# A four-layer graph network on one core: halves of sums added on VectorE, plain transposes, and layer 1 as one stream

## The chip, the cores and the metric

The kernel runs on one core of a Trainium2 chip. The metric is the device time of one execution in microseconds (us). Before the change it is 849.05 us, the median of 3 runs (848.39 to 849.23). The profiled execution took 848.55 us; its trace spans 846.8 us at a mean granted TensorE clock of 0.988.

## The reference

There are 4096 nodes with 64 features, a 4096 x 4096 adjacency matrix of zeros and ones, and four layers. Each takes the normalised, rectified features and adds something aggregated over the neighbours.

```python
# layer 0: the last 100 neighbours of a row, each weighted by a power of 0.5
support = h @ weight
rank = jnp.cumsum(mask, axis=1); deg = rank[:, -1:]
k = jnp.minimum(deg, 100.0); pos = rank - (deg - k)
x = x + (mask * jnp.where(pos > 0, 0.5 ** (k - pos), 0.0)) @ support + bias
# layer 1: attention over the neighbours
h = lorentz_linear(h, W, b, scale)          # time = sigmoid(h[:, :1])*exp(scale)+1.1, rest rescaled
q = lorentz_linear(h, Wq, bq, scale_q); k = lorentz_linear(h, Wk, bk, scale_k)
qm = jnp.concatenate([-q[:, :1], q[:, 1:]], axis=-1)
att = adj * jax.nn.sigmoid((2.0 + 2.0 * (qm @ k.T)) / att_scale + att_bias)
support = att @ h
x = x + support / jnp.sqrt(clip(abs(-inner(support)), 1e-8))
# layer 2: two gated steps, each with m = adj @ (x @ W), then r, z, n as in a GRU
# layer 3: A @ (gamma * X) and A @ (gamma - 1) with hyperbolic rescaling before and after
# every layer: h = jnp.maximum(_layernorm(x), 0.0), and x = x + layer(h, adj)
```

## The kernel before

The adjacency matrix is held on chip transposed, in one-byte floats (`A8`), which is exact for zeros and ones. The output nodes are treated in four quarters `q` of 1024 nodes, each in two chunks `c` of 512; the sum over the source nodes runs over 32 blocks `b` of 128. A value of the features is split into three bf16 parts. The first two lie side by side in `hm` (128 columns), the third in `lo` (64 columns). A product with `hm` uses the full array, one with `lo` half of it ("tiled"); so one bank of sums holds two halves of 64 rows that must still be added.

TensorE's order is laid down when the program is built. A helper (`weave`) keeps a clock for each engine, and puts pre- and post-processing of other quarters (generators that `yield` one instruction after the other) in between the large products. It also draws on a background list: `checks`, VectorE instructions that test every half tile (128 x 512) of the adjacency in 32-bit form for values other than 0 and 1, by a separate load.

```python
def evac(acc, bias=None):                       # both banks to the on-chip buffer
    a = [b2(f"agg{c}", (P, CW)) for c in (0, 1)]
    if bias is None:
        S_.activation(a[0], acc[0], AF.Copy)
        V.tensor_copy(a[1], acc[1])
    else:
        S_.activation(a[0], acc[0], AF.Identity, bias=bias)
        V.tensor_scalar(a[1], acc[1], bias, None, op0=ALU.add)
    ...
def to_nm(a, kind):                             # to rows of nodes; adds the halves
    def half(ps, c):
        ps = bank(kind, "ps_n") if ps is None else ps
        for j in range(CB):                     # both = two 64x64 identities, one on the other
            mm(ps[:, (c * CB + j) * D:(c * CB + j + 1) * D], a[c][:, j * P:(j + 1) * P], both)
        return ps
    ps = yield PE([a[0]], lambda: half(None, 0), 0.8, [kind])
    yield PE([a[1]], lambda: half(ps, 1), 0.8)

# pre1(q): the queries, each block twice, so that both halves of the array find them
ys = [b2("q", (P, CB, 2, D)) for _ in range(2)]
for c in range(2):
    yield from stretch(hq, tm[:, QB:], f[:, QB:], ys[c], slice(c * CB, (c + 1) * CB), -1.0)
kT[q] = b2(f"kT{q}", (P, CW))
yield from transpose4(y, 1, kT[q])
for c in range(2):
    qd = b2("qd", (P, CW))
    yield from transpose4(ys[c].rearrange("p b t d -> p (b t) d"), 1, qd)
    ...                                         # and to DRAM

def stream1(q):                                 # layer 1, one quarter
    acc = [one(f"acc{c}") for c in (0, 1)]
    ...  # weigh(i, c): 2 score products, sigmoid on ScalarE, times A8 on VectorE
    behind = None
    for i in range(NB // 2):
        gs = []
        for c in (0, 1):
            gs.append(weigh(i, c)); weave.draw(c == 1 or weave.quiet)
        for c in (0, 1):
            if behind: add(c, *behind)          # the sums of the step before
            weave.draw(weave.quiet)
        behind = (i, gs)
        if i == 8: load1(q + 1)                 # the queries of the next quarter
    weave.finish()
    for c in (0, 1): add(c, *behind)
    return acc

def sum2(acc, layer, q, bs):                    # layer 2, eight blocks
    for b in bs:
        for c in (0, 1): add_hm(acc, layer, b, c, a8(q, b)(c), b == 0)     # full width
        weave.draw()
    for b in bs:
        for c in (0, 1): add_lo(acc, layer, b, c, a8(q, b)(c), b == NB - 1)  # half width
        weave.draw(False)
```

Layer 2 already takes the even blocks of nodes as one chunk and the odd ones as the other (`a8`), and adds the halves by `take2`: a copy of one half by ScalarE (`mt`), an addition by VectorE (`mx`). Layers 0 and 1 take the first and the last 512 nodes as chunks.

Of the kernel before, what the change touches and what calls it, by code (L numbers as in the profile page):

```python
# [790 lines left out]
def fast_kernel(ctx: ExitStack, tc: tile.TileContext, t: dict, out: bass.AP, flag: bass.AP):  # L791
# [76 lines left out]

    both = const.tile([P, D], F32, name="both")
    V.tensor_tensor(both, ident[:, :D], ident[:, D:], ALU.add)  # L870
# [66 lines left out]
    def book_pe(o, lhsT, rhs, passes):  # L937
        k, m, n = lhsT.shape[0], math.prod(lhsT.shape[1:]), math.prod(rhs.shape[1:])
        tiled = k < P or m < P
        dur = max(0.42e-3 * n * passes * (0.5 if tiled else 1.0), 0.09 * (2.0 if passes == 4 else 1.0))  # L940
        weave.book("P", dur + (0.115 if tiled != weave.tiled else 0.0), names(lhsT, rhs), names(o))
        weave.tiled = tiled
# [60 lines left out]
    def add_hm(acc, layer, b, c, rhs, first):  # L1003
        o = like(acc[c], rhs)
        mm(o, HM[layer, b // QB][:, b % QB, :], rhs, start=first, stop=False)
# [5 lines left out]
    def evac(acc, bias=None):  # L1011

        a = [b2(f"agg{c}", (P, CW)) for c in (0, 1)]
        if bias is None:
            S_.activation(a[0], acc[0], AF.Copy)
            V.tensor_copy(a[1], acc[1])
        else:
            S_.activation(a[0], acc[0], AF.Identity, bias=bias)
            V.tensor_scalar(a[1], acc[1], bias, None, op0=ALU.add)
        for ps in acc:  # L1020
            free(ps)
        return a

    def to_nm(a, kind):

        def half(ps, c):
            ps = bank(kind, "ps_n") if ps is None else ps
            for j in range(CB):
                mm(ps[:, (c * CB + j) * D:(c * CB + j + 1) * D], a[c][:, j * P:(j + 1) * P], both)
            return ps  # L1030
        ps = yield PE([a[0]], lambda: half(None, 0), 0.8, [kind])
        yield PE([a[1]], lambda: half(ps, 1), 0.8)
        return blocks(ps)

# [71 lines left out]
    def stream0(q):  # L1106
# [5 lines left out]
        def turn(b):  # L1112

            n = q * NB + NB - 1 - b
            a = A8[q][b // 2][:, b % 2, :]
            wt = b2("w", (P, 2 * CW), I16)
            for c in (0, 1):
                if b < NB - 1:
                    before = A8[q][(b + 1) // 2][:, (b + 1) % 2, :]
                    mm(cnt[c], upd, before[:, cols[c]], start=False, stop=False)  # L1120
                mm(cnt[c], tri, a[:, cols[c]], start=b == NB - 1, stop=b == 0)
# [35 lines left out]
        for b in range(1, NB, 2)[::-1]:  # L1157
# [18 lines left out]
            if b == NB // 2 + 1:  # L1176
                xq[q] = b2(f"x{q}")
                Y_.dma_start(xq[q], x_nm[:, q * QB:(q + 1) * QB, :])
        for x in cnt:
            free(x)  # L1180
        while waiting:
            for _ in sums():
                weave.draw()
# [38 lines left out]
    def stretch(h, tm, f, o, s, sign):  # L1222

        n, k = o.shape[1], o.shape[2]
        yield root[0].tensor_scalar(o[:, :, :, 0], tm[:, s, None].to_broadcast([P, n, k]), sign, None, op0=ALU.mult)
        yield DV.tensor_tensor(o[:, :, :, 1:], h[:, s, None, 1:].to_broadcast([P, n, k, D - 1]),
                               f[:, s, None, None].to_broadcast([P, n, k, D - 1]), ALU.mult)

    def pre1(q, X):
# [10 lines left out]
        every = slice(0, QB)  # L1240
        S1[q] = b2(f"S1_{q}")
        tm, f = yield from lorentz([hs], [es[:, 0:1]])
        yield from stretch(hs, tm, f, S1[q][:, :, None, :], every, 1.0)
# [17 lines left out]
        yield from stretch(hk, tm[:, :QB], f[:, :QB], y[:, :, None, :], every, 1.0)  # L1261
        ys = [b2("q", (P, CB, 2, D)) for _ in range(2)]
        for c in range(2):
            yield from stretch(hq, tm[:, QB:], f[:, QB:], ys[c], slice(c * CB, (c + 1) * CB), -1.0)
# [3 lines left out]
        for c in range(2):  # L1268
            qd = b2("qd", (P, CW))
            yield from transpose4(ys[c].rearrange("p b t d -> p (b t) d"), 1, qd)  # L1270
            q_spill[q, c] = dram.tile([P, CW], F32, name=f"qs{q}_{c}")
            yield AC.dma_start(q_spill[q, c], qd)
# [3 lines left out]
    def load1(q):  # L1276
        if q < NQ:
            qd[q] = [b2("qd", (P, CW)) for _ in range(2)]
            for c in range(2):
                Y_.dma_start(qd[q][c], q_spill[q, c])  # L1280

    def stream1(q):

        acc = [one(f"acc{c}") for c in (0, 1)]

        def weigh(i, c):
            kb = kT[i // 4][:, (i % 4) * P:(i % 4 + 1) * P]
            ps = two("score").rearrange("p (j n) -> p j n", j=2)
            for j in range(2):
                half = slice(j * D, (j + 1) * D)  # L1290
                mm(ps[:, j, :], kb[half, :], qd[q][c][half, :])
            g = b4p.tile([P, 2, CW], F32, tag="b4", name="sig")
            S_.activation(g, ps, AF.Sigmoid, bias=att_add, scale=att_mul)
            free(ps)
            V.tensor_tensor(g, g, A8[q][i][:, :, c * CW:(c + 1) * CW], ALU.mult)
            return g

        def add(c, i, gs):
# [5 lines left out]
        behind = None  # L1304
        for i in range(NB // 2):
            if q == 0 and i % (QB // 2) == 0:
                weave.until((1, i // (QB // 2)), DONE)
            weave.quiet = (1, NQ - 1) not in DONE
            weave.late = 2.0 if weave.quiet else 1.0
            gs = []  # L1310
            for c in (0, 1):
                gs.append(weigh(i, c))
# [495 lines left out]
```

## Time and profile before

| what | before |
|---|---|
| time, median of 3 | 849.05 us |
| layer 0 | from the start to 249.6 us |
| layer 1, four quarters | 252.3 to 517 us |
| layer 2, two steps | 518 to 727 us |
| layer 3 products | 727 to 821.8 us |
| rest after the last product of layer 3 | 25.0 us |
| VectorE busy in layer 1, one inner quarter | 54.4 of 64.4 us |

A line of the profile that tells of a group has the line of the program (here mostly a helper's), the engine, the operation, output and inputs by name, then shapes, and a count after "x". After the bar stand busy time in us and mean ns of one, then idle time of the engine before such instructions and who ended it. PE is TensorE, DVE VectorE, ACT ScalarE; PEld is the load of weights, which overlaps products. For TensorE the product's own duration is longer than the time until the next can start; what it costs in a row is seen from start to start. A 32-bit product makes two records, a transpose one.

### The profile page before, as it was taken

To read this page: it belongs to the slowest core of one execution; us is meant where nothing else is said; L and a number is where in the kernel's file an instruction comes from. 1 tells how busy PE (TensorE), PEld (TensorE's weight loads), DVE (VectorE), ACT (ScalarE), POOL (GpSimd) and SP (SyncE) were. 2 spreads that over 40 slices of the span, in tenths; PEclk is the share of its full clock that TensorE was granted. 3 is DMA by queue.
4 is the path that set the end of the run, shared out by engine and by line. 5 is a ranking of instruction groups with operands and counts; after the bars stand their busy time and mean duration, and the time that the engine had idled before them with its cause. 6 is when DMAs were issued, how large, how long until landed. Compare 5 with 4: busy or idle time off the path is not lost.

```text
span 846.8 us, 12798 instructions
## 1 busy us (share of the span) xinstructions
PE 803.9 (95%) x4682; PEld 378.5 (45%) x4682; DVE 644.0 (76%) x1670; ACT 397.8 (47%) x609; POOL 69.5 (8%) x143
## 2 busy tenths in 40 slices
PE   5999999999998999999999999999999999999980
PEld 2434434444442333333333334444444444699980
DVE  6725766667667888888888888977678788885996
ACT  5654555555546666666666663022210234452342
POOL 4333322322000000000000000000000000000000
PEclk9999999999999999999999999999999999999995
DMA  9999999999641041032022133796778920000010
GB/s 133 114 141 161 161 198 205 149 176 204 131 138 36 14 148 51 13 101 63 12 88 63 37 112 137 260 308 194 257 251 299 313 58 13 1 2 2 14 26 17
DMA packets 67752, 101.63 MB, mean 120 GB/s; under 512 B 18785, under 2 KB 35169, under 8 KB 67681
## 3 DMA queue, kind: packets, MB, share of 16 engines
q1 hardware_dynamic: 46800, 79.18, 29.9%
q0 software_dynamic: 18432, 16.79, 21.0%
q10 hardware_dynamic: 2448, 4.76, 1.6%
q8 instruction: 39, 0.64, 0.3%
q14 instruction: 33, 0.26, 0.1%
HBM read 144.75 MB, written 6.29 MB: 178 GB/s over the span
## 4 chain that ended last, share of the span: by engine, by line
PE 86%; DVE 7%; DMA 2%; ACT 2%; issue 1%; POOL 0%; POOLq 0%; ACTq 0%; DVEq 0%
PE acc L947 50%; PE score L947 14%; PE cnt L947 13%; PE ps_l L947 2%; PE ps_t L951 2%; PE rz L947 2%; DMA half<-in_adjT 2%; PE ps_n L947 2%; PE ih L947 1%; DVE sig L780 1%; DVE n L780 1%; DVE nt L780 1%; DMA A<-in_adjT 1%; PE ps_kq L947 1%; DVE rc L780 1%
## 5 line engine op out<-in xcount | busy, mean ns | idle before, releaser
L780 ACT ACTIVATE sig<-score,fatt_add,fatt_mul 128x1024 f32<-128x1024 f32 x128 | 147.6, 1199 | 86.3 <-PE score L947 85.6
L780 DVE TENSOR_TENSOR sig<-sig,A 128x1024 f32<-128x1024 f32 x128 | 151.3, 1221 | 37.1 <-ACT sig L780 36.6
L780 ACT ACTIVATE w<-cnt 128x512 int16<-128x512 f32 x192 | 108.1, 595 | 95.9 <-PE cnt L947 93.8
L947 PE MATMUL score<-qd,kT 64*128 64x512 f32 x512 | 128.0, 616 | 2.1 <-ACT sig L780 2.1
L947 PE MATMUL acc<-sig,S 128*64 128x512 f32 x512 | 125.1, 606 | 1.1 <-DVE sig L780 0.8
L947 PE MATMUL acc<-A,hm 128*128 128x512 fp8e4 x512 | 117.5, 380 | 0.9 <-DVE X L780 0.9
L947 PEld LDWEIGHTS <-hm 128*128 128x128 bf16 x768 | 72.4, 98 | 94.1 <-issue 18.4
L947 PE MATMUL cnt<-A,ftri 128*128 128x512 fp8e4 x256 | 98.1, 386 | 7.9 <-DMA A<-in_adjT 7.9
L780 DVE SCALAR_TENSOR_TENSOR half<-half 128x512 f32<-128x512 f32 x150 | 98.3, 683 | 2.6 <-DMA half<-in_adjT 2.6
L947 PE MATMUL cnt<-A,fupd 128*128 128x512 fp8e4 x248 | 95.6, 385 | 4.3 <-ACT w L780 2.1
L947 PE MATMUL acc<-S,A 128*128 128x196 bf16 x1024 | 88.5, 247 | 0.0
L947 PEld LDWEIGHTS <-A 128*128 128x128 fp8e4 x1024 | 87.2, 97 | 1.5 <-issue 1.0
L780 DVE TENSOR_SCALAR w<-cnt 128x512 int16<-128x512 f32 x64 | 44.2, 690 | 50.9 <-PE cnt L947 49.8
L947 PEld LDWEIGHTS score<-qd,kT 64*128 64x128 f32 x512 | 43.8, 186 | 79.5 <-ACT sig L780 36.9
L1104 POOL DMA_DIRECT2D A<-in_adjT x128 | 67.7, 531 | 138.5 <-DMA A<-in_adjT 135.1
L947 PE MATMUL acc<-w,hm 128*128 128x512 bf16 x256 | 75.1, 379 | 0.0
L947 PEld LDWEIGHTS acc<-sig,S 128*64 128x64 f32 x512 | 30.3, 136 | 83.2 <-issue 30.4
L780 DVE SCALAR_TENSOR_TENSOR whole<-whole 128x1024 f32<-128x1024 f32 x53 | 63.5, 1219 | 4.9 <-DMA whole<-in_adjT 4.3
L947 PEld LDWEIGHTS <-lo 128*64 128x64 bf16 x768 | 35.4, 109 | 59.8 <-issue 40.1
L947 PE MATMUL acc<-A,lo 128*64 128x512 fp8e4 x512 | 61.3, 382 | 0.0
L1561 POOL MEMSET S<- 128x4 bf16 x8 | 0.9, 119 | 545.5 <-DVE xT L780 481.0
L947 PEld LDWEIGHTS <-fupd 128*128 128x128 bf16 x248 | 24.6, 99 | 43.7 <-issue 21.7
(180 smaller groups left out, 724.2 us busy)
## 6 DMA issues: line engine op xcount, KB each, us to landing
half<-in_adjT SPq DMA_DIRECT2D x150, 256.0 KB, 6.6
whole<-in_adjT SPq DMA_DIRECT2D x53, 512.0 KB, 6.4
A<-in_adjT POOLq DMA_DIRECT2D x128, 128.0 KB, 12.7
x<-in_x SPq DMA_DIRECT2D x8, 256.0 KB, 16.1
qs<-qd ACTq DMA_DIRECT2D x8, 256.0 KB, 5.7
qd<-qs SPq DMA_DIRECT2D x8, 256.0 KB, 2.7
mx<-gs SPq DMA_DIRECT2D x16, 128.0 KB, 7.3
xT<-gs SPq DMA_DIRECT2D x8, 256.0 KB, 7.1
```

What stands on the lines that cost most here:

```text
L780: return fn(*args, **kw)
L947: nc.tensor.matmul(o, lhsT, rhs, start=start, stop=stop, skip_group_check=True)
L951: nc.tensor.transpose(o, src, ident)
L1104: nc.gpsimd.dma_start(A8[q][b // 2][:, b % 2, :], adjT[b * P:(b + 1) * P, q * 2 * CW:(q + 1) * 2 * CW])
L1561: nc.gpsimd.memset(S3[q, c][:, :, 3 * e:], 1.0)
```

## The change

Six things are changed, mostly to take work and waits from TensorE.

1. The halves of the sums of layers 0 and 1 are added as in layer 2: ScalarE copies the other half of each bank, VectorE adds. One tile holds both chunks, one in the upper and one in the lower 64 partitions, so four plain 128 x 128 transposes bring it to rows of nodes.
2. For that, layers 0 and 1 take even and odd blocks as chunks too.
3. The queries are turned once, not twice; the load from DRAM puts them on both halves of the partitions.
4. In layer 2 a piece of eight blocks starts with the half-width products if the array is in that tiling, to change it less often.
5. Layer 1 is one stream over its four quarters: the first scores of a quarter are issued before the last sums of the one before, and those of the first quarter before the last sums of layer 0.
6. The helper's own clock gets other figures for transposes, 32-bit products and changes of tiling.

```diff
     def evac(acc, bias=None):
-        a = [b2(f"agg{c}", (P, CW)) for c in (0, 1)]
-        if bias is None:
-            S_.activation(a[0], acc[0], AF.Copy)
-            V.tensor_copy(a[1], acc[1])
-        else:
-            S_.activation(a[0], acc[0], AF.Identity, bias=bias)
-            V.tensor_scalar(a[1], acc[1], bias, None, op0=ALU.add)
-        for ps in acc:
+        lo, hi = slice(0, D), slice(D, P)
+        a, mt = b2("agg", (P, CW)), b2("mt", (P, CW))
+        sides = ((lo, hi), (hi, lo))
+        for ps, (own, other) in zip(acc, sides):
+            S_.activation(mt[own, :], ps[other, :], AF.Copy)
+        for ps, (own, other) in zip(acc, sides):
+            if bias is None:
+                V.tensor_tensor(a[own, :], ps[own, :], mt[own, :], ALU.add)
+            else:
+                V.scalar_tensor_tensor(a[own, :], ps[own, :], bias[own, :], mt[own, :], op0=ALU.add, op1=ALU.add)
             free(ps)
     def to_nm(a, kind):
+        def run():
+            ps = bank(kind, "ps_n")
+            for j in range(4):
+                turn4(ps[:, j * P:(j + 1) * P], a[:, j * P:(j + 1) * P])
             return ps
+        ps = yield PE([a], run, 0.7, [kind])
 ... # stream0: a8(q, b) in place of columns c * 512 ...; before its last sums, in the last quarter:
+        if q == NQ - 1:
+            begin1()                    # weigh(0, 0, c) for both c, kept in `ahead`
 ... # pre1
-        ys = [b2("q", (P, CB, 2, D)) for _ in range(2)]
-        for c in range(2):
-            yield from stretch(hq, tm[:, QB:], f[:, QB:], ys[c], slice(c * CB, (c + 1) * CB), -1.0)
+        yq = b2("q")
+        yield from stretch(hq, tm[:, QB:], f[:, QB:], yq, -1.0)
 ...
+        qT = b2("qT", (P, CW))
+        yield from transpose4(yq, 1, qT)
 ... # load1
-                Y_.dma_start(qd[q][c], q_spill[q, c])
+                for half in (slice(0, D), slice(D, P)):
+                    Y_.dma_start(qd[q][c][half, :], q_spill[q][c * D:(c + 1) * D, :])
 ... # stream1
+        for q in range(NQ):
+            for i in range(NB // 2):
+                ...
+                gs = ahead[:] if (q, i) == (0, 0) else []
+                for c in range(len(gs), 2):
+                    gs.append(weigh(q, i, c))
+                    weave.draw(c == 1 or weave.quiet)
+                if behind:
+                    add_behind()        # after step 15: weave.finish(), evac, post1 of that quarter
+                behind.append((q, i, gs))
+        add_behind()
 ... # sum2: wide(stop) and narrow(stop) are the two loops of before
+        if weave.tiled and bs[0]:
+            narrow(False)
+            wide(True)
+        else:
+            wide(False)
+            narrow(True)
 ... # the helper's clock
-        dur = max(0.42e-3 * n * passes * (0.5 if tiled else 1.0), 0.09 * (2.0 if passes == 4 else 1.0))
-        weave.book("P", dur + (0.115 if tiled != weave.tiled else 0.0), names(lhsT, rhs), names(o))
+        dur = max(0.42e-3 * n * passes * (0.5 if tiled else 1.0), 0.09)
+        if passes > 1 and not tiled:
+            dur += 0.05 if passes == 2 else 0.075
+        weave.book("P", dur + ((0.18 if passes == 4 else 0.115) if tiled != weave.tiled else 0.0), ...)
```

## The prediction

> **What bounds the kernel now.** I read the page's busy times and its chain first, then the waits of TensorE, then the groups by shape, and last the timeline around every place that the change touches.
>
> ```profile
> PE 803.9 (95%) x4682; PEld 378.5 (45%) x4682; DVE 644.0 (76%) x1670; ACT 397.8 (47%) x609; POOL 69.5 (8%) x143
> PE 86%; DVE 7%; DMA 2%; ACT 2%; issue 1%; POOL 0%; POOLq 0%; ACTq 0%; DVEq 0%
> ```
>
> ```profile
> PE flag_ps L947 <- DVE odds L780: 18.5, 1, 18.5
> PE cnt L947 <- DMA A<-in_adjT: 7.9, 1, 7.9
> PE cnt L947 <- ACT w L780: 2.1, 7, 0.6
> ```
>
> TensorE is busy for 803.9 of 846.8 us. Its one long wait is at the end: its last sum of layer 3 ends at 821.8 us, and then 25 us of VectorE work (two last post-processings) remain. Before that it idles for 18 us in all, 7.9 of them at the start for the first adjacency block. So before 821.8 us a microsecond of TensorE work removed is a microsecond gained, if no wait takes its place, and the last 25 us stay. Here is what the pieces cost (mean ns after the busy time):
>
> ```profile
> L947 PE MATMUL ps_n<-both,agg 128*128 128x64 f32 x128 | 16.0, 277 | 1.5 <-ACT agg L780 1.5
> L951 PE MATMUL ps_t<-fident,q 128*128 128x128 f32 x32 | 4.9, 274 | 0.0
> L780 ACT ACTIVATE agg<-acc,W 128x512 f32<-128x512 f32 x4 | 2.7, 687 | 8.1 <-PE acc L947 8.1
> L780 DVE TENSOR_TENSOR mx<-acc,mt 64x512 f32<-64x512 f32 x16 | 11.0, 689 | 3.0 <-ACT mt L780 2.6
> L780 ACT ACTIVATE mt<-acc 64x512 f32<-64x512 f32 x16 | 9.5, 591 | 64.0 <-PE acc L947 63.6
> L780 DVE TENSOR_TENSOR q<-hq,f 128x504 f32<-128x504 f32 x8 | 5.4, 676 | 0.0
> ```
>
> Now a border between two quarters of layer 1 (start, length):
>
> ```profile
> 319.57 3.99 PE L947 MATMUL acc<-sig,S 128*64 128x512 f32 x16
> 323.49 1.99 PE L947 MATMUL score<-qd,kT 64*128 64x512 f32 x8
> 325.41 2.00 PE L947 MATMUL ps_n<-both,agg 128*128 128x64 f32 x16
> 327.33 1.99 PE L947 MATMUL score<-qd,kT 64*128 64x512 f32 x8
> ```
>
> A normal pair of steps is 1.92 us of scores and 1.87 of sums. The two groups of sums at the seam take 323.49 - 319.57 = 3.92 instead of 3.74: the seam costs 0.18 us, not a round trip through ScalarE and VectorE, because the sums of step 14 cover it. What is dear there is the 1.92 us of ps_n. The border between layers 0 and 1 is different:
>
> ```profile
> 249.00 0.62 PE L947 MATMUL acc<-w,lo 128*64 128x512 bf16 x4
> 250.40 2.00 PE L947 MATMUL ps_n<-both,agg 128*128 128x64 f32 x16 [0.77 <-ACT agg L780]
> 254.60 0.63 ACT L780 ACTIVATE sq<-xc 128x512 f32<-128x512 f32 x1 [4.26 <-DVE xc L780]
> 255.14 4.72 ACT L780 ACTIVATE sig<-score,fatt_add,fatt_mul 128x1024 f32<-128x1024 f32 x4
> 256.38 2.22 PE L947 MATMUL score<-qd,kT 64*128 64x512 f32 x8 [2.06 <-ACT sig L780]
> 259.39 2.21 PE L947 MATMUL acc<-sig,S 128*64 128x512 f32 x8 [0.79 <-DVE sig L780]
> ```
>
> TensorE has nothing to overlap with here: 0.77 + 2.06 + 0.79 = 3.62 us of it stand idle. Last, what a tiling change costs, in layer 0:
>
> ```profile
> 125.72 0.38 PE L947 MATMUL acc<-w,hm 128*128 128x512 bf16 x1
> 126.03 0.62 PE L947 MATMUL acc<-w,lo 128*64 128x512 bf16 x4
> 126.59 0.39 PE L947 MATMUL cnt<-A,fupd 128*128 128x512 fp8e4 x1
> ```
>
> A full-width product is followed by the next after 0.216 us; by a half-width one after 0.31. The way back costs as much: two pairs of half-width products would be 0.43 to 0.47 us and take 0.56. I take 0.1 us per change.
>
> **What the Trainium skill says.** "TensorEngine Tiling (Array Packing)", section "Tiling Modes", says that changing the tiling mode drains TensorE; the 0.31 against 0.216 above agrees. "TensorE: Matmul & The Clock Gate", section "Part 4: PE-mode transpose", gives about 275 ns for a 128x128 transpose inside a kernel; the records here say 274. But four in a row start 0.109 us apart, so the four hold TensorE for 0.44 us, and it is this that I count. "PSUM — Partial Sum Buffer", section "Specifications (TRN2)", says that a VectorE instruction may take at most one tensor input from PSUM: this is why adding two halves of a bank takes a copy by ScalarE first. No run here tests it; the trace shows layer 2 doing it in that way (mt, then mx). "DMA: Bandwidth & Descriptors", section "Rules for kernel authors", advises against splitting a transfer into two partition halves, because they serialize. The queries are now loaded so. The two loads of before land after 2.7 us and are asked for 8 steps (30 us) ahead, so I give this no cost.
>
> **The change part by part.**
>
> *Halves added on VectorE, plain transposes.* Per aggregate 16 ps_n records go. They hold TensorE for 1.84 us next to full-width work and for 1.92 us between half-width work. Four transposes come, 0.44 us, or about 0.52 with the change of tiling. This is 1.4 us for each of eight aggregates. The evacuation grows: instead of 0.69 on ScalarE beside 0.75 on VectorE, two copies of 0.59 on ScalarE and two adds of 0.69 on VectorE, the first add behind the first copy. From the end of the sum to the finished tile it is 0.6 + 0.7 + 0.7 = 2.0 us instead of 0.75. In layers 1 and 2 other products fill this: 4 x 1.4 = 5.6. At the end of layer 0 scores fill it: 1.4. At the three inner seams of layer 0 I expect most to be lost. There the next quarter starts with one block in flight, and its counts need the same two engines to empty the banks. At the seam at 190 us the first w leaves ScalarE at 191.7 and would now leave at 192.3; that of VectorE leaves at 192.0 and would leave at 193.1. Count products that started at 193.13 would start at 192.4 and 193.2, and the third block, which began at 194.41, at about 193.7, then stall once and take in the 0.44 of transposes. I count 0.35 x 3 = 1.0. Sum: 8.0 us.
>
> *Queries turned once.* Per quarter one set of four transposes less, three times 0.44 in layer 0 and once 0.52 in layer 1: 1.85 us. VectorE loses 4 x (0.68 + 0.17) and ScalarE 4 x 0.60; they are not the bound.
>
> *Start of layer 1.* The scores of the first step (8 records, 1.9 us) are issued before the last sums of layer 0, so their sigmoid and multiplication run under 1.5 us of sums and the next scores. Of 3.62 us idle I expect 3.0 back. Part may return: ScalarE's sq waited 4.26 us for VectorE ahead of the sigmoids, and this normalisation still has to be fitted in.
>
> *Seams inside layer 1.* 3 x 0.18 = 0.5 us. The fourth seam, after the last quarter, stays.
>
> *Fewer tiling changes in layer 2.* There are 2 steps x 4 quarters x 4 pieces = 32 pieces, each now wide-narrow, so nearly 2 changes a piece. Alternating, one stays inside each piece and most of the 31 between pieces go; eight pieces with block 0 must start wide, and gates and transposes in between force some. I take 20 changes x 0.1 = 2.0 us.
>
> *Even and odd blocks as chunks.* Layer 2 already streams this strided view at 0.216 us a product, so TensorE pays nothing. VectorE's multiplication reads A in runs of 128 instead of 512; I take it as unchanged at 1.22 us.
>
> Sum: 8.0 + 1.85 + 3.0 + 0.5 + 2.0 = 15.35 us, so 849.05 - 15.35 = 833.7 us.
>
> **Rivals.** (1) *The checks spill into the tail.* VectorE also tests all 256 half tiles of the adjacency for values other than 0 and 1, in gaps, at 0.61 us each. Layer 1 gets shorter and VectorE's own work grows by about 2 us (adds +5.3, queries -3.4), so some 10 checks move later. What is left at the end lies in the last 25 us: 10 left would cost 6 us, hence 840. Against it: before, checks are all but finished by 717 us, one 1.2 us and one 0.7 us piece remain, and the 200 us of layer 2 have VectorE 79% busy, so there is room. (2) *The seams of layer 0 get worse*: copies and adds ahead of the count evacuations on both in-order engines. If each seam loses 1 us instead of gaining 0.35, the time is 838. For it: the counts already wait 0.25 us there. Against: only the first two blocks are exposed. (3) *The start of layer 1 gains all and more*: with the two products ahead, the later single waits vanish too, and layer 0 loses its stray waits (1.78 us at 109 us). This makes 829 to 830. (4) *VectorE becomes the bound of layer 1*: 54.4 us of 64.4 in a quarter now, about 55 of 62.7 after; the checks give way first, so I think this unlikely; it would show as 835 to 838.
>
> **Range and chances.** 2% is 832.1 us, only 1.6 us below my number. The terms are each sure to about 1 us except the start of layer 1 and layer 0's seams (1.5 each), and program order moves everywhere, so stray waits of 1 to 2 us come and go. Range 828.5 to 839. Faster by over 2%: 0.32; within: 0.65; slower: 0.03.
>
> **What would show it.** ps_n as 32 transposes of 128x128 with some 4 us of TensorE in place of 16; records for q halved to 16; scores of layer 1 standing before the last lo products of layer 0; no gap of 2 us near 255; a full-width run of 32 hm products in layer 2; a quarter of layer 1 at about 62.7 us instead of 64.4; the last layer 3 product at about 806.5. I am wrong if checks stand in the last 25 us in number, if TensorE waits over 1 us at each layer 0 seam, or if multiplications of layer 1 take clearly more than 1.22 us.

## The result and the profile after

The changed kernel takes 839.36 us (median of 4 runs, 838.91 to 840.59), the kernel before beside it 849.14 us (848.39 to 850.65). The ratio is 0.9885, with a 95% interval of 0.9867 to 0.9902. The change saves 9.8 us; 15.35 were predicted, and 839.36 lies 0.4 us above the predicted range.

The page after, first the busy times, then the chain by engine:

```profile
PE 786.7 (94%) x4549; PEld 368.7 (44%) x4570; DVE 648.4 (77%) x1675; ACT 400.8 (48%) x613; POOL 69.5 (8%) x143
PE 82%; DVE 9%; DMA 5%; ACT 2%; issue 1%; SPq 0%; DVEq 0%
```

TensorE lost 17.2 us of busy time (803.9 before), more than was predicted (a few products are missing in this trace: 4549 against 4570 weight loads), but its share of the chain fell from 86 to 82% and that of DMA rose from 2 to 5%. So part of the removed work came back as waiting. The groups by shape show that the operations themselves changed as foreseen:

```profile
L780 DVE SCALAR_TENSOR_TENSOR agg<-acc,W,mt 64x512 f32<-64x512 f32 x8 | 6.0, 749 | 9.2 <-ACT mt L780 9.1
L950 PE MATMUL ps_n<-fident,agg 128*128 128x128 f32 x32 | 5.1, 281 | 0.0
L950 PE MATMUL ps_t<-fident,q 128*128 128x128 f32 x16 | 2.5, 276 | 0.0
```

ps_n is now 32 transposes, and the query transposes are halved to 16. The multiplication of layer 1 (`sig<-sig,A`), which now reads A in runs of 128, takes 1222 ns instead of 1221. To see where the gain is and where it isn't, I cut both traces at the same events: layer 0 ends with the start of its last count product, layer 1 with the first product of layer 2, layer 2 with the first of layer 3, layer 3 with the start of its last product; the tail is the rest.

| stage, us | before | after | difference | predicted |
|---|---|---|---|---|
| layer 0 | 247.0 | 252.2 | +5.2 | -2.3 |
| layer 1 | 269.6 | 262.6 | -7.0 | -9.6 |
| layer 2 | 210.9 | 204.6 | -6.3 | -3.4 |
| layer 3 | 94.1 | 93.9 | -0.2 | 0 |
| tail | 25.2 | 24.6 | -0.6 | 0 |

(The predicted column is the prediction's sum by place: in layer 0 the three seams, 1.0, and three query sets, 1.32; in layer 1 the 1.4 at its border, 3 of the 4 aggregates, 4.2, the start, 3.0, one query set, 0.5, and the seams, 0.5; in layer 2 the last aggregate, 1.4, and the tilings, 2.0.)

Layer 0 is where the largest surprise lies: it got longer. The waits of TensorE and of VectorE between 60 and 252 us, in the trace after (total, number, longest):

```profile
PE cnt L946 <- DVE w L780: 5.5, 2, 4.0
PE cnt L946 <- ACT w L780: 5.4, 7, 1.4
DVE half L780 <- DMA half<-in_adjT: 7.9, 3, 4.8
```

Before, the same three were 1.8, 1.4 and 2.6 us. The first and the third belong together, as the timeline after shows (start, length, in brackets the idle time before and who ended it):

```profile
112.24 0.69 DVE L780 SCALAR_TENSOR_TENSOR half<-half 128x512 f32<-128x512 f32 x1 [4.83 <-DMA half<-in_adjT]
...
112.86 0.69 DVE L780 TENSOR_SCALAR w<-cnt 128x512 int16<-128x512 f32 x1
```

```profile
113.60 0.59 PE L946 MATMUL cnt<-A,fupd 128*128 128x512 fp8e4 x1 [4.02 <-DVE w L780]
```

`half` is one of the background tests of the adjacency (`checks`, counted in half tiles below). VectorE kept to the order of the program here. It stood at a test whose load had not landed, and the evacuation `w` of a count bank stood behind it: TensorE's last product before had ended at 109.58 us, but `w` began at 112.86. TensorE waited 4.02 us for that bank. The granted clock went down with it; by the trace it was half from 112.15 to 118.97 us. Here are the window of 5 us with the stop in it and the next one (PEclk is the third number from the right, then DMA share and GB/s):

```profile
110.00:115.00 5.00, 1.04 (x4) 0.29 (x5) 2.13 (x6) 0.62 (x2) 1.05 (x2) 0.71 1.10 200
115.00:120.00 5.00, 5.00 (x16) 1.61 (x16) 3.16 (x15) 1.20 (x3) 1.58 (x3) 0.60 1.10 201
```

From 115 to 120 us TensorE never rests and finishes 16 products; before, at the same place, 29. The kernel before has the same stop in small (VectorE 2.59 us, TensorE 1.78 us at 109 us) and no drop of the clock after it. The DMA queues are full in both (share 1.10 in these windows). The two loads of tests on the chain after take 16.5 and 17.5 us, the one on the chain before 14.5 us.

The three inner seams of layer 0 show the second wait of the list:

```profile
70.07 1.21 ACT L780 ACTIVATE mt<-acc 64x512 f32<-64x512 f32 x2 [3.16 <-PE acc L946]
...
71.30 0.60 ACT L780 ACTIVATE w<-cnt 128x512 int16<-128x512 f32 x1
...
71.95 0.38 PE L946 MATMUL cnt<-A,fupd 128*128 128x512 fp8e4 x1 [1.37 <-ACT w L780]
```

The two copies of the evacuation occupy ScalarE ahead of the first `w`, and TensorE waits 1.37 us for it at each seam.

The start of layer 1:

```profile
253.32 1.99 PE L946 MATMUL score<-qd,kT 64*128 64x512 f32 x8
...
256.21 0.62 PE L946 MATMUL acc<-w,lo 128*64 128x512 bf16 x4
...
307.33 0.66 PE L950 MATMUL ps_t<-fident,k 128*128 128x128 f32 x4 [2.15 <-DVE k L780]
```

The scores stand before the last sums of layer 0, and the three waits of before (0.77, 2.06 and 0.79 us) are gone. But at step 12 of the first quarter, 50 us later, TensorE waits 2.15 us for `k`: the keys of the last quarter of nodes, which come out of the last sums of layer 0 by way of its post-processing and the normalisation of layer 1. In the trace before this wait does not exist.

Layer 2 after; each line is a run of full-width (hm) or half-width (lo) products:

```profile
582.51 3.64 PE L946 MATMUL acc<-A,lo 128*64 128x512 fp8e4 x32
586.09 7.08 PE L946 MATMUL acc<-A,hm 128*128 128x512 fp8e4 x32
```

Runs of 32 take the place of runs of 16: the trace has 42 changes of tiling in the whole of layer 2 instead of 70.

### The profile page after: what moved, and what is told of

It reads as the page before. It is cut to its first block, busy times and chain, and to the rows that moved or that the text cites. A ratio compares the mean times of both kernels' runs of the same rounds, so it can differ in the third digit from the quotient of the medians.

```text
span 837.9 us, 12661 instructions
## 1 busy us (share of the span) xinstructions
PE 786.7 (94%) x4549; PEld 368.7 (44%) x4570; DVE 648.4 (77%) x1675; ACT 400.8 (48%) x613; POOL 69.5 (8%) x143
## 4 chain that ended last, share of the span: by engine, by line
PE 82%; DVE 9%; DMA 5%; ACT 2%; issue 1%; SPq 0%; DVEq 0%
PE acc L946 50%; PE score L946 13%; PE cnt L946 11%; DMA half<-in_adjT 4%; PE ps_l L946 2%; DVE sig L780 2%; PE rz L946 2%; PE ih L946 2%; PE ps_t L950 1%; DVE nt L780 1%; DVE n L780 1%; DMA x<-in_x 1%; DVE ss L780 1%; ACT w L780 1%; ACT sig L780 1%
## 5 line engine op out<-in xcount | busy, mean ns | idle before, releaser
L780 DVE TENSOR_TENSOR sig<-sig,A 128x1024 f32<-128x1024 f32 x128 | 151.3, 1222 | 33.0 <-ACT sig L780 32.6
L946 PE MATMUL acc<-A,hm 128*128 128x512 fp8e4 x512 | 115.6, 379 | 0.0
L780 DVE SCALAR_TENSOR_TENSOR half<-half 128x512 f32<-128x512 f32 x156 | 101.5, 686 | 8.0 <-DMA half<-in_adjT 7.9
L946 PE MATMUL acc<-w,hm 128*128 128x512 bf16 x235 | 69.9, 382 | 0.7 <-issue 0.2
L946 PEld LDWEIGHTS <-lo 128*64 128x64 bf16 x768 | 36.9, 109 | 58.5 <-issue 36.7
L780 DVE SCALAR_TENSOR_TENSOR whole<-whole 128x1024 f32<-128x1024 f32 x50 | 59.8, 1219 | 3.0 <-DMA whole<-in_adjT 2.6
L946 PE MATMUL acc<-A,lo 128*64 128x512 fp8e4 x512 | 59.3, 380 | 0.0
L780 ACT ACTIVATE mt<-acc 64x512 f32<-64x512 f32 x32 | 18.9, 591 | 65.6 <-PE acc L946 65.2
L946 PEld LDWEIGHTS <-ftri 128*128 128x128 bf16 x256 | 25.0, 99 | 48.8 <-issue 26.9
```

The source lines that it names most:

```text
L780: return fn(*args, **kw)
L946: nc.tensor.matmul(o, lhsT, rhs, start=start, stop=stop, skip_group_check=True)
```

## The experiments

Three questions: do the tests take the gain back; what are the waits of layer 0 and of the start of layer 1 worth; and what do the single parts bring. The theory I began with was *room*: the 256 half tiles need a fixed amount of VectorE time, VectorE is busy for 225 of 262.6 us in layer 1 after (86%; before 224 of 269.6, 83%) and for 167 of 204.6 in layer 2 (82%), so time taken out of these layers takes room from the tests, and they are paid for in layer 0 or in the tail. The rival was that the change's own waits eat the gain, tests or no tests. The stages of the runs, with the tests that lie in each:

| run | time, us | layer 0 | layer 1 | layer 2 | tail | tests in layers 0, 1, 2, tail |
|---|---|---|---|---|---|---|
| before | 849.14 | 247.0 | 269.6 | 210.9 | 25.2 | 63, 42, 148, 3 |
| after | 839.36 | 252.2 | 262.6 | 204.6 | 24.6 | 74, 39, 143, 0 |
| b2_nochecks0 | 881.67 | 244.8 | 269.9 | 209.6 | 61.6 | 0, 44, 154, 58 |
| a2_nochecks0 | 885.75 | 244.9 | 263.8 | 205.7 | 75.6 | 0, 34, 144, 78 |
| b0_none | 841.85 | 244.8 | 268.5 | 208.2 | 24.4 | none |
| a0_none | 832.71 | 243.7 | 263.7 | 204.0 | 24.8 | none |
| a3_land | 861.32 | 245.8 | 263.8 | 205.8 | 50.4 | 40, 35, 140, 41 |
| a12_hl78 | 838.82 | 245.3 | 263.7 | 205.8 | 28.8 | 67, 37, 146, 6 |
| a10_late_hland | 841.51 | 243.0 | 263.2 | 205.7 | 33.9 | 63, 35, 144, 14 |
| a9_late_aland | 840.61 | 244.0 | 263.2 | 205.7 | 31.7 | 65, 35, 144, 12 |
| a6_late | 844.24 | 252.3 | 263.2 | 205.7 | 28.1 | 74, 34, 144, 4 |
| a1_oldclock | 842.76 | 247.2 | 264.8 | 206.5 | 29.1 | 69, 35, 147, 5 |
| a4_nobegin | 841.82 | 251.0 | 265.4 | 204.7 | 24.5 | 74, 39, 143, 0 |
| a11_keys | 841.85 | 250.8 | 259.6 | 205.6 | 28.9 | 74, 32, 144, 6 |
| a11n_keys_none | 828.46 | 244.0 | 259.5 | 204.0 | 24.9 | none |
| a5_oldsum2 | 841.79 | 252.2 | 262.6 | 207.6 | 24.7 | 74, 39, 143, 0 |
| a7_oldhalves | 844.53 | 249.3 | 267.1 | 206.8 | 25.9 | 67, 43, 145, 1 |
| a13_gp | 868.40 | 244.1 | 299.5 | 205.2 | 23.4 | 63, 37, 136, 0 (20 on GpSimd) |

Layer 3 takes 93.9 to 94.6 us in all of them. The stages come from one profiled execution each, the times are medians; b2 and a2 have one time each. The kernel before, run again beside each group of runs, has medians of 848.58 to 850.28 us. Where the interval of a run's ratio overlaps that of the changed kernel (a1, a4, a5, a9, a10, a11 and a12), the difference between their times is not clear of noise, and the stages carry the reading.

### Both kernels with the tests starting only at the end of layer 0

```diff
-        if q == 0:
+        if q == NQ - 1:
             weave.add(checks(), back=True)
```

> The kernel before, with the background checks of the adjacency started only in the last quarter's end of layer 0 instead of after the first quarter. Layer 0 (first count to last count) took 239.1 us with them. Theory 'late checks' (check loads that land late hold VectorE in front of the count evacuations): the single wait of 1.78 us at 109 us goes, layer 0 is 1 to 3 us shorter, about 237. Rival 'VectorE's new adds': the same, as there are none in this kernel. The whole gets longer, as 64 half checks move to later; that is not what is read here.

> The changed kernel with the same late start of the checks. Its layer 0 took 244.1 us with them, 5.0 us more than before. Theory 'late checks': without them the waits of 4.02 and 1.49 us and the lower clock after the first go, and layer 0 is 1.5 to 2.5 us SHORTER than that of the kernel before in the same state, about 235. Rival 'VectorE's new adds and ScalarE's new copies at the seams': layer 0 stays 3 to 5 us longer than that of the kernel before in the same state, about 241.

Without tests in layer 0 the two kernels need the same time for it, 244.8 and 244.9 us: so the 5.2 us that layer 0 lost against before are a matter of tests, not of TensorE's work. Counted from the first count product, as in the expectations, it is 236.9 and 236.4 us (239.1 and 244.1 with tests): the shorter layer 0 of the theory, but by 0.5 us only. In layers 1 and 2 the changed kernel takes in 178 tests instead of 198, and 78 instead of 58 are left for the tail, which costs 14 us more. That is what *room* says: the layers that became shorter hold fewer tests.

### Both kernels without the tests

```diff
-        todo = [(b, c) for c in range(NQ) for b in range(NB)]
+        todo = []
```

These two leave out the test of the adjacency's values altogether.

> The kernel before without any check of the adjacency for other values than 0 and 1 (it leaves that part out; the rest is unchanged). VectorE loses 256 half checks of 0.61 us. From the late-start run, whose last layer 3 product began at 818.2 us, and the tail of 25 us: 840 to 844.

> The changed kernel, also without any check. Theory 'room for the checks': the shortfall against the predicted 15 us lies in the checks, which lost room in layers 1 and 2 and crowd layer 0; without them the change is worth 13 to 15 us, so 826 to 829. Rival 'PE path': the gain on TensorE's own path was over-estimated (late-start runs: 818.2 against 808.3), and the change is worth 9 to 11 us without checks too, so 831 to 834.

Measured: before 841.85 us (ratio 0.9913, 0.9896 to 0.9929), after 832.71 us (0.9807, 0.9791 to 0.9824). The tests cost the kernel before 7.3 us (849.14 - 841.85) and the changed one 6.7 us (839.36 - 832.71). Without any tests the change is worth 9.1 us, no more than with them. So *room*, as the reason for the missing 6 us, fell: the tests moved, and where they are paid for moved from layers 1 and 2 to layer 0 (they cost 2.2, 1.1 and 2.7 us in layers 0, 1 and 2 before, and 8.5, -1.1 and 0.6 after), but their sum is nearly the same. What is missing is missing without tests too: of a predicted 2.3 us in layer 0 there are 1.1, and of a predicted 9.6 in layer 1 there are 4.8. In layer 1 of a0_none one sees where. Windows from 300 to 308 us:

```profile
300.00:304.00 4.00, 3.98 (x11) 1.25 (x12) 0.74 (x1) 2.10 (x4) 0.00 (x0) 0.57 0.63 197
304.00:308.00 4.00, 4.00 (x20) 1.25 (x18) 1.78 (x3) 2.24 (x3) 0.00 (x0) 1.00 0.00 0
```

The wait for the last keys is there as well, 2.15 us long and up to 298.74 us, and here the clock falls to 0.57 after it: 11 products in 4 us instead of 20.

### The late loads of layer 0

The helper decides when to draw a test from a reckoned landing time of its load. a3 reckons twice as long for a load of half a tile, a12 and a10 a little longer. a6, a9 and a10 also allow the pre- and post-processing of layer 1's start to be placed so that it holds TensorE up by 3 us instead of 2 in the helper's reckoning (as long as the last keys are outstanding; no tests are drawn in that time), and a9 reckons more for the adjacency's own blocks in place of the half loads.

```diff
-                w.land(k, 1.4 if "whole" in k else 0.7)
+                w.land(k, 1.4)                             # a3_land
+                w.land(k, 1.4 if "whole" in k else 0.78)   # a12_hl78
+                w.land(k, 1.4 if "whole" in k else 0.85)   # a10_late_hland
...
-        weave.late = 2.0 if weave.quiet else 1.0
+        weave.late = 3.0 if weave.quiet else 1.0           # a6_late, a9_late_aland, a10_late_hland
...
-        weave.land(A8[q][b // 2].tensor.name, 1.4)
+        weave.land(A8[q][b // 2].tensor.name, 1.5)         # a9_late_aland
```

> The changed kernel, but the helper reckons 1.4 instead of 0.7 us for the transfer of a half check, so that it places each check later after its load. Theory 'late checks': waits of VectorE for check loads in layer 0 fall from 7.9 to under 2 us, the clock stays at 1.00, layer 0 is 5 to 6 us shorter and the whole takes 833 to 836. Rival 'the seams': layer 0 stays at 244, the whole 838 to 841.

> The changed kernel, in which the chain to the last keys may hold up a sigmoid or a multiplication of layer 1's first steps by up to 3 us instead of 2. Theory 'chain': the keys come 2 us earlier or more, the wait at step 12 falls under 1 us, 836.5 to 838.5. Rival: the chain is bound by its own instructions, or every hold-up makes TensorE wait in the first steps: 839 to 842.

> As the run with 3 us, and the helper reckons 1.5 instead of 1.4 us for the transfer of an adjacency block in layer 0, so that the checks there are placed later. Theory 'late checks': waits of VectorE for check loads in layer 0 fall from 8 us to under 3 and layer 0 is 4 us shorter; some 5 to 10 checks move on, and those which find no room in layers 1 and 2 cost 0.63 us each at the end. 832 to 838. Rival 'checks are a fixed sum': what layer 0 gains the end loses, 838 to 841.

> As the run with 3 us, and the helper reckons 0.85 instead of 0.7 us for the transfer of a half check. Theories as for the run before: 832 to 838 if layer 0's waits go and few checks are left at the end; 838 to 842 if the end loses what layer 0 gains. Every check left at the end counts 0.63 us.

> The changed kernel, whose helper reckons 0.78 us for the transfer of a half check, between its 0.7 and the 0.85 of the run before. If the checks are a fixed sum that layer 0's waits and the end share, the best lies between: some 6 checks left at the end (4 us) against 7 us of layer 0, 836 to 839. If any step up from 0.7 leaves a dozen checks, 840 to 842.

VectorE's waits for loads of tests in layer 0 fall from 7.9 us to none (a3, a9, a10) and 1.5 us (a12), the clock stays at 1.00, and layer 0 becomes 6.4 to 9.2 us shorter: the late loads are shown to be what made it long. But the times are 861.32 us (ratio 1.0145, 1.0128 to 1.0162), 840.61 (0.9891, 0.9873 to 0.9908), 841.51 (0.9905, 0.9880 to 0.9929) and 838.82 (0.9856, 0.9816 to 0.9897). What is not tested in layer 0 is tested after the last product of layer 3: 41 tests for 25.8 us more of tail in a3, 14 for 9.3 in a10, 12 for 7.1 in a9, 6 for 4.2 in a12, so 0.6 to 0.7 us each. The tail of a3, by groups of VectorE:

```profile
L780 DVE SCALAR_TENSOR_TENSOR whole<-whole 128x1024 f32<-128x1024 f32 x15 | 18.2, 1222 | 1.6 <-DMA whole<-in_adjT 1.3
L780 DVE SCALAR_TENSOR_TENSOR half<-half 128x512 f32<-128x512 f32 x11 | 7.0, 686 | 0.0
```

Here *room* is right: a test costs VectorE its 0.61 to 0.69 us somewhere, and the only question is whether TensorE waits for it. a12 has the lowest median of all kernels that do the whole work, but its interval overlaps that of the changed kernel, so no difference is shown. a6 alone (844.24, 0.9926, 0.9909 to 0.9942) leaves the waits of layer 0 as they are (7.9 us) and adds 3.5 us of tail. The last keys come sooner, 46.2 us after the last sums of layer 0 instead of 50.4, and at step 12 it has no wait. But the timeline of its layer 1 has several others, of up to 1.55 us, the last long one of them

```profile
299.03 2.21 PE L946 MATMUL acc<-sig,S 128*64 128x512 f32 x8 [0.92 <-DVE sig L780]
```

and its layer 1 is 263.2 us long, 0.6 more than after. Moving the wait is not removing it.

### The helper's old clock

```diff
-        dur = max(0.42e-3 * n * passes * (0.5 if tiled else 1.0), 0.09)
-        if passes > 1 and not tiled:
-            dur += 0.05 if passes == 2 else 0.075
-        weave.book("P", dur + ((0.18 if passes == 4 else 0.115) if tiled != weave.tiled else 0.0), ...)
+        dur = max(0.42e-3 * n * passes * (0.5 if tiled else 1.0), 0.09 * (2.0 if passes == 4 else 1.0))
+        weave.book("P", dur + (0.115 if tiled != weave.tiled else 0.0), ...)
```

> The changed kernel with the helper's clock as it was before. Theory 'the new figures let more checks into layer 0' (77 against 64): about 64 to 66 checks run in layer 0, the wait at 109 us is back to some 1.8 us, and the time is 833 to 836. Rival 'the order of the change itself does it': 77 checks or the same waits, 838 to 841.

842.76 us (0.9923, 0.9901 to 0.9945), 3.4 us slower than the changed kernel (the intervals just touch). Layer 0 is 5.0 us shorter, with 69 tests in it and 4 us of waiting for loads instead of 7.9; layers 1 and 2 are 2.2 and 1.9 us longer, and 5 tests are left for the tail (29.1 us). So the new figures lengthen layer 0, but they are not to blame for the shortfall of the whole: what they cost there is gained behind it. Of the 11 tests that layer 0 holds more than before (74 against 63; the 77 and 64 of the expectation count up to its last sums), 5 come with the new figures. Where the other 6 come from I did not take apart, and it stays open.

### The start of layer 1

a4 leaves out the early scores. a11 cuts the dependence that makes step 12 wait: the last four steps of the first quarter take keys and values of the first quarter of nodes in place of the last, so the result of that quarter of nodes is another one; a11n does so and leaves the tests out too.

```diff
-        if q == NQ - 1:
-            begin1()                                        # a4_nobegin
...
-                if q == 0 and i % (QB // 2) == 0:           # a11_keys, a11n_keys_none
+                if q == 0 and i % (QB // 2) == 0 and i < 12:
                     weave.until((1, i // (QB // 2)), DONE)
-        kb = kT[i // 4][:, (i % 4) * P:(i % 4 + 1) * P]
+        kb = kT[0 if q == 0 and i > 11 else i // 4][:, (i % 4) * P:(i % 4 + 1) * P]
-                mm(..., S1[b // QB][:, b % QB, :], ...)
+                mm(..., S1[0 if q == 0 and i > 11 else b // QB][:, b % QB, :], ...)
```

> The changed kernel without the early scores: the first scores of layer 1 stand after the last sums of layer 0 again. Theory 'chain': layer 1 can't pass its step 12 before the keys of the last quarter are transposed, some 51 us after the last sum of layer 0 whatever TensorE does, so what is gained at the start is given back as the wait of 2.15 us there. Without the early scores the first steps come 2 to 3 us later, the wait at step 12 falls under 0.5 us, and the time is the same within 1 us: 838.4 to 840.4. Rival 'the start's gain is real': the wait at step 12 stays and the time is 3 us longer, 842 to 843.

> The changed kernel, whose first quarter of layer 1 takes keys and values of source quarter 0 in its steps 12 to 15 in place of those of source quarter 3 (other values, same work), so that it need not wait for the last chain. Theory 'chain': the wait of 2.15 us at step 12 goes and nothing takes its place, the stretch from the last count to the first product of layer 2 falls from 262.6 to about 260.4 us, 836.5 to 838. Rival 'VectorE's load in the first quarter' (chain and multiplications together, as in the run with 3 us, where the waits only moved): the stretch stays within 0.7 us of 262.6, 838.7 to 840.

> The same without any check of the adjacency. Theory 'chain': the wait of 2.15 us and the lower clock after it (1.6 us) go, and from 832.7 the time falls to 828.5 to 830, 12 to 13 us under the kernel before without checks (841.9). Rival 'VectorE's load in the first quarter': 831.5 to 833.

a4 takes 841.82 us (0.9904, 0.9885 to 0.9923). If the chain to the last keys had set the end of step 12 alone, dropping the early scores would have cost nothing. It cost 2.8 us in layer 1, but not at the border: there TensorE waits for only 0.61 us (3.62 before). The chain itself grew, from 50.4 to 53.8 us between the end of layer 0's last sums and the last write of the keys, and with it the wait at step 12; behind that the clock was halved for 3.4 us, which it was not in the changed kernel. Why the chain is longer in this order stays open.

```profile
256.16 2.23 PE L946 MATMUL score<-qd,kT 64*128 64x512 f32 x8 [0.61 <-ACT sig L780]
...
307.61 1.06 PE L950 MATMUL ps_t<-fident,k 128*128 128x128 f32 x4 [4.03 <-DVE k L780]
```

By these traces the early scores are worth something, but not as the 3.0 us of idle time at the border that I had booked: the rest of the change removes most of that without them. a11 shows what the chain takes. Its step 12 in layer 1:

```profile
305.63 1.94 PE L946 MATMUL acc<-sig,S 128*64 128x512 f32 x8
307.50 0.66 PE L950 MATMUL ps_t<-fident,k 128*128 128x128 f32 x4
308.52 1.99 PE L946 MATMUL score<-qd,kT 64*128 64x512 f32 x8
```

The keys are no longer waited for. Of the layer's waits 0.99 us for `sig` at 267.67 us is left; it takes 259.6 us, 3.0 less than after, and without tests 259.5, 4.2 less than a0_none (there the drop of the clock goes too). Without tests the whole time is 828.46 us (0.9738, 0.9699 to 0.9777): against b0_none the change is worth 13.4 us then, near the 15.35 predicted. With tests, a11 takes 841.85 us (0.9916, 0.9895 to 0.9938), no better than the changed kernel: its layer 1 holds 32 tests instead of 39, layer 2 is 1.0 us longer, and 6 tests stand in a tail of 28.9 us, 4.3 more. Without tests the wait for the last keys, with the clock behind it, is the largest missing term, 4.2 of 6 us. With tests, taking that wait away buys nothing: the tests that the shorter layer no longer holds are paid for behind it. Whether another order of the tests could keep the 3.0 us isn't shown.

### The order of the sums in layer 2, and the halves

a5 gives layer 2 its old order. a7 brings back the products with two identities (`both`) for the halves, on even and odd chunks; as both halves now carry layer 0's bias, it counts that bias twice.

```diff
-        if weave.tiled and bs[0]:
+        if False:                                           # a5_oldsum2
             narrow(False)
...
-            S_.activation(mt[own, :], ps[other, :], AF.Copy) # a7_oldhalves: evac and to_nm of before
+            mm(ps[:, (2 * j + c) * D:(2 * j + c + 1) * D], a[c][:, j * P:(j + 1) * P], both)
```

> The changed kernel with layer 2's order of before (full width, then half width, in each piece). Layer 2 has 42 changes of tiling in the changed kernel and 70 before. At 0.1 us a change layer 2 grows from 204.6 by 2.8 us, and the time from 839.4 to about 842; by the prediction's 2.0 us to 841.4. Rival 'layer 2's gain came from lost waits': under 1 us.

> The changed kernel with the halves of layers 0 and 1 added by products with two identities again, 16 records each, and the evacuation of before; chunks, queries, order and the stream of layer 1 stay. By the prediction's terms this costs 8 us: 5.6 + 1.4 in layer 1 and at its borders, 1.0 at layer 0's seams, so 847. Theory 'room for the checks': VectorE also gets 5 us of its time back and TensorE's longer layer 1 gives room, so the checks wait less and it is only 3 to 5 us slower, 842 to 844.

a5: 841.79 us (0.9909, 0.9893 to 0.9926), 2.4 us slower than the changed kernel, and its layer 2 is 3.0 us longer; nothing else moves. With 28 changes of tiling between the two orders this is 0.1 us per change, as estimated. a7: 844.53 us (0.9936, 0.9917 to 0.9955), so the halves bring 5.2 us (4.3 by the ratios) of the 8.0 I gave them. They bring 4.5 in layer 1 and 2.2 in layer 2, and 2.9 us go back in layer 0, where the changed kernel has 7 tests more and waits 7.9 us for loads instead of 4.3.

### Twenty of the tests on GpSimd

GpSimd is all but idle after layer 0. It tests 20 half tiles from the start of layer 1 on; half loads are reckoned as in a10.

```diff
+            yield GP.tensor_scalar(v, a, 1.0, None, op0=ALU.is_equal)
+            yield GP.tensor_tensor(v, a, v, ALU.subtract)
+            yield GP.tensor_scalar(v, v, 0.0, None, op0=ALU.is_equal)
+            yield GP.tensor_tensor(good, good, v, ALU.mult, saturate=False)
...
+    weave.add(checks_gp(), back=True)
     stream1()
```

> The changed kernel with 0.85 us for the transfer of a half check, and GpSimd takes 20 of the 256 half checks from the start of layer 1 on, each by four plain instructions (equal to 1, subtract, equal to 0, multiply into a running product). Theory 'checks want room on VectorE': layer 0 stays free of waits for check loads (243 to its last count), the 14 checks left at the end go, and the time is 831 to 835, below the changed kernel. Rival: GpSimd's instructions slow VectorE or TensorE waits for them: 839 or more.

868.40 us (1.0215, 1.0173 to 1.0258). The tail is short at last (23.4 us), but layer 1 takes 299.5 us, 36.9 more. The groups of its page by shape, and then VectorE's multiplication in the 15 us from 340 on, where GpSimd is at work:

```profile
L780 POOL TENSOR_SCALAR gt<-ghalf 128x512 f32<-128x512 f32 x20 | 43.1, 2155 | 87.9 <-DVE tm L780 82.6 <-PE ps_t L950 5.1
L780 POOL TENSOR_TENSOR gt<-ghalf,gt 128x512 f32<-128x512 f32 x20 | 33.7, 1686 | 1.7
L780 DVE TENSOR_TENSOR sig<-sig,A 128x1024 f32<-128x1024 f32 x128 | 181.9, 1461 | 21.8 <-ACT sig L780 21.5
```

```profile
L780 DVE TENSOR_TENSOR sig<-sig,A 128x1024 f32<-128x1024 f32 x6 | 10.1, 1726 | 0.0
```

The multiplication takes 1726 ns there instead of 1221, and it is on TensorE's path: the waits of TensorE for `sig` in layer 1 are 20.1 us in this run, and one more of 7.6 us is for a tile of ScalarE. From 500 us on, with GpSimd done, it takes 1221 ns again. The Trainium skill, "SBUF — State Buffer", section "Who interferes with whom", says that a VectorE instruction with two inputs from SBUF contends with a GpSimd instruction that reads SBUF. This multiplication has two such inputs, and the run agrees. But it is not the whole of the 36.9 us. In layer 1 ScalarE waits 20.0 us for GpSimd instructions by the trace, and TensorE's stop of 7.6 us is behind one of these waits:

```profile
391.11 0.60 ACT L780 ACTIVATE gT<-ps_t 128x512 f32<-128x512 f32 x1 [9.87 <-POOL good L780]
```

In the program the large tiles of all engines, `gT` and GpSimd's own among them, take turns in the same 24 buffers (`b2`), so a tile can have to wait until GpSimd is done with its buffer. This would explain these waits, but no run with separate buffers shows it.

## Why the prediction was wrong, step by step

*Halves and transposes, 8.0 us.* 5.2 in the reverse experiment. The count of TensorE's work was right: inner quarters of layer 1 take 62.8 us instead of 64.35 (62.7 predicted). What failed is the 1.0 us "at the three inner seams of layer 0", and what the change set off there. TensorE waits 1.37 us for `w` and does 0.44 us of transposes, where it waited 0.24 and did 1.84. Between the first count products of a seam and the first full-width sum behind it, a0_none takes 4.74 us and b0_none 4.87: the seam gains 0.13 us, not 0.35. The prediction's own warning, a wait of over 1 us at each seam, came true without the loss that rival 2 gave it.

*Queries turned once, 1.85 us.* Three sets of 0.44 in layer 0: without tests layer 0 gained 1.1 us in all, with the seams (0.4) and a first quarter that ends 0.6 us later (69.67 against 69.04 us). The term itself is right as far as this sum shows; it was not tried alone. The load in two halves costs nothing that the trace shows: a half lands after 2.7 us in the median, as the whole did before, and TensorE has no wait for `qd`.

*Start of layer 1: "Of 3.62 us idle I expect 3.0 back."* This step failed, and without tests it is most of what is missing. The idle time at the border is gone, but the steps are not a free run behind it. Step 12 needs the last quarter's keys, which come some 50 us after the last sums of layer 0 (256.8 to 307.3 us after, 248.2 to 298.7 us in a0_none), by a chain that the change doesn't shorten (49.5 us before, 50.4 after). The prediction said "Part may return" and looked for it in the first sigmoids; it came back at the end of the chain instead, as 2.15 us, with 0.99 us for `sig` on the way. Together with the halved clock behind it, that wait takes 4.2 us without tests (a0_none against a11n_keys_none). Nor is the cure what the prediction took it for: without the early scores (a4) TensorE is idle for only 0.61 us at the border. I read the chain of the kernel before only where it had a wait, and not what the next wait behind it would be.

*Layer 0 without a term.* With tests this is the largest miss, 7.5 us. That layer 0 would lose 5.2 us stands in no part of the sum. Rival 1 had the mechanism of the tests right (fixed work, paid where VectorE is scarce), but looked for it in the tail. In the changed kernel the tail is clean (24.6 us); the price was paid in layer 0, where more tests are drawn while the DMA queues are full, their loads land late, and an in-order VectorE passes the wait on to TensorE. The prediction saw the stray wait of 1.78 us at 109 us and thought it might vanish; it grew to 4.02 us and took the clock with it.

*Seams inside layer 1, 0.5 us.* Inner quarters gained 1.53 us where 1.4 (transposes against ps_n) and 0.18 (seam) were expected: right.

*Tiling changes in layer 2, 2.0 us.* The mechanism and the 0.1 us were right, the number was too small: 28 fewer, not 20, and 3.0 us by the reverse experiment. Another 1.3 us came from waits of TensorE in layer 2 that vanished (1.34 us idle before, 0.03 after; without tests layer 2 gained 4.2 = 1.4 + 2.8). So layer 2 gave 2.9 us more than predicted, against the 7.5 us by which layer 0 missed: it is luck that the whole came within 5.6 us of the prediction, and without it some 842 us would have been measured.

*Tail, layer 3.* 24.6 us against 25 predicted. The last product of layer 3 starts at 813.3 us, not at 806.5; without tests at 806.0. Rival 4 (VectorE as the bound of layer 1) is not seen: VectorE is 86% busy there, and TensorE's waits in the layer are 1.5 and 2.2 us.

## What to carry to other kernels

When waiting time is taken out at the start of a stage, follow the longest chain that feeds a later step of that stage, and ask when TensorE would arrive there: what comes sooner may only wait longer. Background work with a fixed total isn't free where its engine has little time to spare (VectorE is 86% busy in layer 1 here); shortening the stage moves it elsewhere, and moving it has to be costed at the place where it arrives. A background instruction must not stand in the program's order before its load will have landed: here everything behind it on VectorE waited as well, and TensorE with it.

## What was not expected of the hardware

**The clock after a stop.** When TensorE stood still for 4.02 us (up to 113.60 us), the clock was halved from 112.15 to 118.97 us; half of the 5.4 us behind the stop, some 2.7 us, is lost on top of it (an estimate). After stops of 1.78 and 2.06 us (before) it stayed at 1.00. After a stop of 2.15 us it was halved for 3.4 us in a0_none (0.57 in the window above) and not at all in the changed kernel. Of the ten traces with a stop of 2.10 to 2.19 us eight show such a drop; after and a5 don't. Nor is its length fixed: the stop of about 4 us in layer 0 was followed by one of 6.8 us in after, a5 and a6 and by one of 3.4 us in a4 and a11, whose layer 0 is 1.2 and 1.4 us shorter. The Trainium skill, "TensorE: Matmul & The Clock Gate", section "Part 1: The HAM clock gate (the "warmup" mystery)", has the clock halve after an idle window of about 3.4 us. The stop of 4.02 us is longer than that, but the clock was halved 2.6 us into it; that of 2.15 us in a0_none is shorter and lost the clock all the same. So a stop of 2 us can be costed neither at its length nor surely above it.

**GpSimd beside VectorE.** One pass of GpSimd over 128 x 512 values in 32 bits takes 1.7 to 2.2 us in the mean, and while it does so VectorE's multiplication goes from 1.22 to 1.73 us: an idle engine was no free help.

**Late loads.** A load of 256 KB for the tests lands after 6.6 us in the median over the whole kernel, but took 16.5 and 17.5 us where it ended a wait in layer 0, with the queues at a share of 1.10.
